# Gated attention: tiles' states side by side in four groups of the array's columns, logits with a block in each half of the columns

## The chip, the cores and the metric

The kernel runs on one core of one Trainium2 chip. The metric is the device time of one execution in microseconds (us); the median of several runs is compared. The core has TensorE (PE, with PEld for its weight loads), VectorE (DVE), ScalarE (ACT), GpSimd (POOL) and SyncE (SP), which issues most DMAs. A tile here is also 128 consecutive tokens; a block is 512 tokens, four tiles.

## The reference, cut to what matters

Two layers are computed, each an attention and a feed-forward part with residuals and layer norms. The change is in the second layer's attention, on 2 sequences of 1024 tokens with 512 channels, keys of 32 and values of 512:

```python
q = jax.nn.softmax(x @ Wq.T, axis=-1)            # [b, L, 32]
k = jax.nn.sigmoid(x @ Wk.T)
gf = jax.nn.log_sigmoid(-k)                       # log of the decay
# in chunks, with Bc the running sum of gf in the chunk:
A = tril(einsum('bid,bjd,bijd->bij', q, k, exp(Bi - Bj)))
o = A @ v + (q * exp(Bc)) @ S                     # v = x
S = S * exp(Blast)[..., None] + einsum('bjd,bjv->bdv', k * exp(Blast - Bc), v)
# then
go = o @ Wog.T + x @ Wig.T
x = layernorm(x + (rmsnorm(o) * go * sigmoid(go)) @ Wo.T)
```

All of it is in float32.

## The kernel before

One program of four stages. Stage 1 (to about 205 us) is the first layer's attention, stage 2 (to about 551 us) its feed-forward part with 4-bit weights, stage 3 (to about 757 us) the gated attention of the second layer, stage 4 its feed-forward part on the tokens that a router picks. The change touches the end of stage 2 and all of stage 3.

A framework turns the Python text into one queue of instructions for each engine: a scheduler orders them by priorities in program order and by its costs, `tc.issue_after(x)` asks that what follows be issued behind `x`, and every queue is then worked off in order, each instruction waiting on semaphores for what it needs. PSUM has eight banks of 128 x 512 floats, used in turn: `mm_bank` gives the next of four, `acc_bank` of the other four. `jk` is a pool with two buffers of 128 x 512 floats, given out in turn under the one tag `junk`; who takes a buffer waits until the readers of what it held are done.

The gated attention works in blocks 0 to 3 (`blk`), two for each sequence `b`:

- `turn(blk)` (L647) transposes the rows of a block on TensorE (`x2Tp`, one bank and one ACT copy a tile) to `xT[blk]`.
- `logits(b)` (L656) multiplies the transposed rows of a sequence's eight tiles with `wqk`, 64 columns (32 for q, 32 for k): eight tiles by four chunks of channels, 32 matmuls with 128 x 128 of `xT` stationary and 64 columns of `wqk` moving, into one bank `lp` (rows on partitions).
- `Gates` (L670) makes from `lp` the sigmoid `k`, the softmax `q`, `l` (negative log decay, by an exponential and a Ln, which need different ACT tables) and, with a matmul by the constant `suf` into `ep`, the decay to the end of a tile, `e`. `decayed` multiplies `e` and `k` to `kd`, written four times side by side (8 tiles x 4 x 32 columns).
- `front(blk)` (L1043) sums `l` along the tokens of four tiles at once by a matmul with `cm` into `cp`; the tiles' 32 key channels stand in the four quadrants of 32 partitions. ACT makes the exponentials `ex`. From the last column of `ex` DVE makes `last`, a matmul with `quads` spreads it over all quadrants (`dp`), and DVE copies the result to `decay`.
- `scores(blk)` (L1060) transposes `q` and `k` (`tp`), weights them on DVE (`km`, `kk`, `qm`, `qk`, `qi`), multiplies them (`sc`, 512 columns, and `sk`, whose stationary operand has 64 columns), masks the result to `A`, and makes the states: for each tile a matmul `up` of the 128 columns of `kd` (four copies of 32) with the tile's rows of `x`, 512 columns, and on DVE `S` = old `S` x `decay` + `up`, 128 x 512. So a tile's state stands in all four quadrants; `qi` of a tile is zero outside the tile's own quadrant.
- `attend(blk)` (L1113) makes the transposed output in four chunks of 128 channels, one bank `op` each: for each tile one matmul of `x` with `A` and one of the tile's `S` with `qi`, 128 columns each (the first tile of a sequence has no `S`). ACT copies each bank to `o` and squares it (`sq`, in a `jk` buffer); POOL adds the squares.
- `o_sum`, `other_sums`, `gate` (L1154) and `finish_by_seven` (L1237) make `go` and the final projection in the seven-product manner (products `go`, `grow`, `P`), `rms` the root mean square (`mp`), `scored_rows` the layer norm and the router's scores; `route` ranks them (`rp`, `cmp`).

The order of the parts is that of the loop at L1637 with `fillers` (L1622), and for the logits of sequence 0 that of the loop that ends stage 2 (`take(pieces, steps)`, the products `P` of the last block, with `turn(1)`, `logits(0)` and `decayed` between). Sequence 1's `turn(3)`, `logits(1)`, `Gates` and `decayed` stand together behind block 1's `rms`.

## Time and profile before

| | |
|---|---|
| median of 3 runs | 976.59 us (975.92 to 977.11) |
| the profiled execution | 977.26 us |
| its span, first to last instruction | 975.5 us |
| TensorE busy, share of the span | 961.5 us, 99% |
| TensorE weight loads | 776.4 us, 80% |
| DVE / ACT / POOL busy | 708.4 / 289.4 / 306.4 us |
| granted TensorE clock, mean | 0.998 |
| `op` matmuls, records: with A, with S | 128 and 112 |
| `lp`, `up`, `dp` matmuls, records | 128, 28, 8 |
| DVE updates of `S` in PSUM and SBUF | 12, median 0.746 us each |

The profile is of one execution, whose time is the span and 1.76 us around it. A matmul on 32-bit floats leaves two records on TensorE and two weight loads, a transposition one of each. The ends of matmuls are modelled and run into the next one, so that the distance from start to start, not the extent, is what a matmul takes of the queue.

### The profile page before, as it was taken

The page shows a single profiled execution, that of the slowest core. Times are in us where ns is not written, and L with a number is a line of the kernel's source. Part 1 is how long each engine was busy: PE and PEld are TensorE (multiplying, and loading weights), DVE is VectorE, ACT ScalarE, POOL GpSimd, SP SyncE. Part 2 cuts the span into 40 slices and gives each one's busy share as a digit, 9 for nine tenths or more (in the row PEclk, how much of TensorE's full clock was granted, in tenths as well). Part 3 has the DMA queues.
Part 4 walks back from the last instruction along what each step waited for, and adds up shares of the span by engine and source line. Part 5 has one row for each costly group of instructions (what it writes and reads, how often), then busy time and mean ns, then how long its engine had stood idle before and what let it go on. Part 6 is the DMA issues. An engine that isn't in the chain of part 4 may idle for free. (4 is left out here: it accounts for less than half of the span.)

```text
span 975.5 us, 11890 instructions
## 1 busy us (share of the span) xinstructions
PE 961.5 (99%) x4437; PEld 776.4 (80%) x4437; DVE 708.4 (73%) x1351; ACT 289.4 (30%) x496; POOL 306.4 (31%) x276
## 2 busy tenths in 40 slices
PE   8999999999999999999999999999999999999996
PEld 6668876775888888888889869969768688888886
DVE  2569986887985686676668386665897795898645
ACT  2244333342552263254242323233121133220000
POOL 1110183004887355575568012001033011000022
PEclk9999999999999999999999999999999999999999
DMA  9622212100000000000020320000004302140011
GB/s 323 209 75 88 88 56 75 53 1 0 2 1 1 1 1 1 1 1 0 1 75 13 136 102 1 2 0 1 1 32 142 130 13 75 44 173 0 1 44 44
DMA packets 25981, 48.88 MB, mean 50 GB/s; under 512 B 4684, under 2 KB 6732, under 8 KB 25411
## 3 DMA queue, kind: packets, MB, share of 16 engines
q1 hardware_dynamic: 23283, 42.98, 13.1%
q0 software_dynamic: 1920, 4.22, 1.1%
q10 hardware_dynamic: 720, 0.92, 0.4%
q8 instruction: 35, 0.57, 0.2%
q14 instruction: 23, 0.19, 0.1%
HBM read 39.70 MB, written 10.52 MB: 51 GB/s over the span
## 5 line engine op out<-in xcount | busy, mean ns | idle before, releaser
L181 POOL TENSOR_TENSOR rs<-rs,table 128x4 f32<-128x4 f32 (+1 forms) x21 | 19.7, 936 | 307.6 <-DVE rs L180 307.4
L741 DVE SCALAR_TENSOR_TENSOR gate<-gatep,scale,gate 128x512 f32<-128x512 f32 x123 | 91.3, 742 | 6.4 <-PE gatep L730 6.1
L741 DVE SCALAR_TENSOR_TENSOR up<-upp,scale,up 128x512 f32<-128x512 f32 x112 | 83.0, 741 | 0.1
L730 PE MATMUL gatep<-x1Th,wgu 128*128 128x512 f32 x176 | 72.5, 412 | 0.6 <-DVE x1Tl L212 0.6
L730 PE MATMUL upp<-x1Th,wgu 128*128 128x512 f32 x176 | 70.4, 400 | 0.1
L730 PE MATMUL upp<-x1Tl,wgu 128*128 128x512 f32 x176 | 68.9, 392 | 0.0
L730 PE MATMUL gatep<-x1Tl,wgu 128*128 128x512 f32 x176 | 68.9, 392 | 0.0
L735 ACT ACTIVATE gate<-gatep,scale 128x512 f32<-128x512 f32 x41 | 28.3, 691 | 110.4 <-PE gatep L730 104.0
L777 PE MATMUL P<-wdn,h 128*128 128x256 f32 x256 | 60.5, 379 | 0.0
L931 POOL TENSOR_TENSOR h<-up,gate 128x512 f32<-128x512 f32 x30 | 38.6, 1287 | 68.6 <-ACT gate L930 63.3
L777 PEld LDWEIGHTS P<-wdn,h 128*128 128x128 f32 x256 | 48.4, 190 | 6.7
L1133 POOL TENSOR_TENSOR sum<-sum,sq 128x512 f32<-128x512 f32 x12 | 17.3, 1442 | 90.7 <-issue 75.9
L1163 PE MATMUL go<-big 128*128 128x256 f32 x192 | 43.4, 380 | 0.0
L367 PE MATMUL xk<-pair,x 128*128 128x512 f32 x96 | 42.7, 592 | 0.0
L730 PEld LDWEIGHTS upp<-x1Th,wgu 128*128 128x128 f32 x176 | 33.0, 187 | 11.7 <-DVE up L741 3.4
L188 DVE BATCH_NORM_STATS2 st<-x 128x6 f32<-128x512 f32 x64 | 42.0, 674 | 0.4
L730 PEld LDWEIGHTS gatep<-x1Th,wgu 128*128 128x128 f32 x176 | 33.1, 188 | 9.2 <-DVE gate L741 1.8
L1163 PEld LDWEIGHTS go<-big 128*128 128x128 f32 x192 | 36.2, 190 | 4.8
L730 PEld LDWEIGHTS upp<-x1Tl,wgu 128*128 128x128 f32 x176 | 33.1, 188 | 6.4 <-issue 0.2
L730 PEld LDWEIGHTS gatep<-x1Tl,wgu 128*128 128x128 f32 x176 | 33.1, 188 | 6.0
L777 PE MATMUL P<-T,S 128*128 128x256 f32 x160 | 36.0, 379 | 0.0
L777 PEld LDWEIGHTS P<-T,S 128*128 128x128 f32 x160 | 30.3, 190 | 4.2
(486 smaller groups left out, 2327.3 us busy)
## 6 DMA issues: line engine op xcount, KB each, us to landing
pk<-in_gu SPq DMA_DIRECT2D x16, 352.0 KB, 3.7
x<-in_x SPq DMA_DIRECT2D x4, 1024.0 KB, 13.1
w<-in_w SPq DMA_DIRECT2D x1, 4096.0 KB, 14.5
xs<-picked SPq DMA_DIRECT2D x4, 1024.0 KB, 5.2
out<-x SPq DMA_DIRECT2D x4, 1024.0 KB, 4.3
w<-in_w SPq DMA_DIRECT2D x4, 1024.0 KB, 7.1
x0T<-in_xT SPq DMA_DIRECT2D x3, 1024.0 KB, 6.2
pk<-in_dn SPq DMA_DIRECT2D x11, 256.0 KB, 3.4
```

The source lines that it names most:

```text
L181: power = nc.gpsimd.tensor_tensor(rs[:, :n], rs[:, :n], const("mhalf")[:, :n], ALU.pow).ins
L188: nc.vector.bn_stats(st, x)
L367: ins = nc.tensor.matmul(acc_of[b][c], x_t[blk][:, i, c * P : (c + 1) * P], pairs_of["k", blk][i // 2][:, i % 2], start=blk % 2 == 0 and i ...
L730: ins = nc.tensor.matmul(ps, wgu[:, k, at * P : (at + 1) * P], x[:, k], start=x is parts[0], stop=x is parts[1]).ins
L735: nc.scalar.activation(acc, ps, AF.Copy, scale=s)
L741: last = nc.vector.scalar_tensor_tensor(acc, ps, s, acc, ALU.mult, ALU.add).ins
L777: last_p[0] = nc.tensor.matmul(cut, x(j)[:, r], w[:, j], start=j == 0, stop=j == NP - 1 and tail is None).ins
L931: hm = nc.gpsimd.tensor_mul(h.chunk(f), up, gate).ins
L1133: nc.gpsimd.tensor_add(sum2, sum2, sq)
L1163: ins = nc.tensor.matmul(ps[:, 256 * m : 256 * m + 256], w[:, k, m], b[:, k, 256 * half : 256 * half + 256], start=first and m == 0 and k ...
```

## The change

- The logits are made transposed: `wqk` (64 columns) is the stationary operand and 512 rows of a block move. The sequence's two blocks stand in the two halves of the array's columns and of one bank's partitions, `lT`, in turn chunk by chunk: 8 matmuls. ACT copies `lT` to SBUF, four transpositions bring it to `lp` (`turned_logits`), with the tiles of a bank in another order, which `Gates` reads by strides.
- `kd` is kept once (8 x 32 columns). A tile's `up` has 32 columns of `kd` stationary and goes to the quadrant of the next tile's number, so that the four (or three) tiles of a block share one bank `up` and stand in the array's four groups of 32 columns.
- A state is kept once, in the quadrant of its tile: `states[blk]` holds the four tiles' states side by side, so that DVE's update works on 32 partitions with the factor read from `ex` in place. `last`, `dp`, `decay` and the constant `quads` are gone. The state before a sequence's first tile is zero (a memset on POOL).
- `attend` multiplies all four tiles' states at once: one matmul of 512 columns for each chunk of channels, in place of four of 128.
- Order: the `ep` matmul moves from `Gates` to `decayed`. At the end of stage 2 the steps of `pieces` are split so that `logits(0)`, `turned_logits`, `Gates` and `decayed` stand further apart. For sequence 1, `turn(3)` moves into block 0's gating, `logits(1)` stands before block 1's `attend`, with `lT` in a `jk` buffer, `turned_logits` and `Gates` right behind it, and `decayed` between the first products of `finish_by_seven`, with `e` in a `jk` buffer. `fillers` is called once, before `sc`, with both halves.

TensorE's queue from the end of `attend`'s block 0 to the `up` of block 2, in words: `tp`, three matmuls `go`, three `up`, five `go`, `sc`, `sk`, 16 `go`, `mp`, 8 `go`, 16 transpositions `x2Tp`, 8 `go`, 8 `lT`, `op` of block 1, 4 `lp`, 4 `grow`, 4 `P`, 8 `go`, `ep`, 4 `grow`, 4 `P`, 8 `go`, 4 `grow`, 4 `P`, 4 `grow`, `mp`, `cp`, `tp`, 2 `go`, 4 `up`.

```diff
@@ -56,7 +56,6 @@
         "one": np.ones((P, 1)),
...
         "mhalf": np.full((P, 4), -0.5),
-        "quads": (tt % 32) == (ii % 32),
     }
...
     for name, a in parts.items():
@@ -653,51 +652,57 @@
             nc.scalar.copy(xT[blk][:, :, i * P : (i + 1) * P], pt.rearrange("p (k t) -> p k t", k=KC))
...
-    def logits(b):
+    def logits(b, room):
+        lT = mm_bank("lT")
+        for k in range(KC):
+            for g in range(2):
+                with tc.issue_after(last_turned[0]):
+                    last_turned[0] = nc.tensor.matmul(
+                        lT[64 * g : 64 * g + 64], wqk[:, k], xT[2 * b + g][:, k], start=k == 0, stop=k == KC - 1
+                    ).ins
+        nc.scalar.copy(room, lT)
+        return room
+    def turned_logits(lT):
         lp = mm_bank("lp")
-        for i in range(8):
-            for k in range(KC):
-                nc.tensor.matmul(
-                    lp[:, i * 64 : (i + 1) * 64],
-                    xT[2 * b + i // 4][:, k, (i % 4) * P : (i % 4 + 1) * P],
-                    wqk[:, k],
-                    start=k == 0,
-                    stop=k == KC - 1,
-                )
+        for i in range(4):
+            last_turned[0] = nc.tensor.transpose(lp[:, i * P : (i + 1) * P], lT[:, i * P : (i + 1) * P], ident).ins
         return lp
...
         def __init__(self, lp, rooms):
-            lg = lp.rearrange("p (i d) -> p i d", d=64)
-            self.q, self.k, self.l, self.e = q, k, l, e = rooms
-            nc.scalar.activation(k, lg[:, :, 32:], AF.Exp, scale=-1.0)
+            lg = lp.rearrange("p (i g d) -> p g i d", g=2, d=64)
+            self.q, self.k, self.l = q, k, l = rooms
+            q4, k4 = (x.rearrange("p (g i) d -> p g i d", g=2) for x in (q, k))
+            nc.scalar.activation(k4, lg[:, :, :, 32:], AF.Exp, scale=-1.0)
             nc.vector.tensor_scalar_add(k, k, 1.0)
...
             red = sp.tile([P, 8], F32, tag="red", name="red")
-            nc.vector.tensor_reduce(red, lg[:, :, :32], AX.X, ALU.max)
-            nc.vector.tensor_sub(q, lg[:, :, :32], red.unsqueeze(2).to_broadcast([P, 8, 32]))
+            red4 = red.rearrange("p (g i) -> p g i", g=2)
+            nc.vector.tensor_reduce(red4, lg[:, :, :, :32], AX.X, ALU.max)
+            nc.vector.tensor_sub(q4, lg[:, :, :, :32], red4.unsqueeze(3).to_broadcast([P, 2, 4, 32]))
             nc.scalar.activation(q, q, AF.Exp)
...
+        def decayed(self, kd, e):
             ep = mm_bank("ep")
-            nc.tensor.matmul(ep[:, :256], const("suf"), l.rearrange("p i d -> p (i d)"), start=True, stop=True)
+            ins = nc.tensor.matmul(
+                ep[:, :256], const("suf"), self.l.rearrange("p i d -> p (i d)"), start=True, stop=True
+            ).ins
             nc.scalar.activation(e.rearrange("p i d -> p (i d)"), ep[:, :256], AF.Exp)
-        def decayed(self, kd):
             self.kd = kd
-            nc.vector.tensor_mul(
-                kd, self.e.unsqueeze(2).to_broadcast([P, 8, 4, 32]), self.k.unsqueeze(2).to_broadcast([P, 8, 4, 32])
-            )
+            nc.vector.tensor_mul(kd, e, self.k)
+            return ins
...
         NP = (NI - 1) // 2
@@ -966,7 +971,7 @@
...
         W1oT = part(3, [4, 512])
-        kd_room, o_room = shaped(8192, [8, 4, 32]), shaped(9216, [KC, 512])
+        kd_room, o_room = shaped(8192, [8, 32]), shaped(9216, [KC, 512])
...
         gA11, gA12, gA21, gA22 = (
@@ -994,18 +999,26 @@
                 pass
...
             with tc.issue_after(mm), tc.issue_after(hm):
-                take(pieces, steps)
+                take(pieces, 3)
+            if n == 3:
+                with tc.issue_after(last_p[0]):
+                    lp = turned_logits(lT)
+                gate_rooms = [
+                    x[:, i * 256 : (i + 1) * 256].rearrange("p (i d) -> p i d", d=32) for x in (b2, rw) for i in range(2)
+                ]
+                gates = Gates(lp, gate_rooms[:3])
+            with tc.issue_after(mm), tc.issue_after(hm), tc.issue_after(last_turned[0]):
+                take(pieces, steps - 3)
             if n < 2:
...
             if n == 2:
-                gates = Gates(logits(0), [
-                    x[:, i * 256 : (i + 1) * 256].rearrange("p (i d) -> p i d", d=32) for x in (b2, rw) for i in range(2)
-                ])
+                lT = logits(0, rooms[1][0])
             if n == 3:
-                gates.decayed(kd_room)
                 sums_of_gate()
             if n == 4:
+                with tc.issue_after(last_p[0]):
+                    gates.decayed(kd_room, gate_rooms[3])
                 x_sum(0)
...
         W1o = place_w(1, "W1o")
@@ -1032,7 +1045,8 @@
     picked = [dram.tile([TOPK, ROW], F32, name=f"picked{b}") for b in range(B)]
...
     index = [cpool.tile([P, 8], I32, name=f"index{b}") for b in range(B)]
-    oT, uT, tri, state, inv = {}, {}, {}, {}, {}
+    oT, uT, tri, states, inv = {}, {}, {}, {}, {}
+    new_state = lambda: wk.tile([P, C], F32, tag="S", name="S", bufs=3)
...
     fronts = {}
@@ -1040,28 +1054,20 @@
     def of_tiles(x, blk):
...
-    def front(blk, gates, before=None):
+    def front(blk, gates):
...
         last_ex[0] = nc.scalar.activation(ex[:, 3], cp[:, :P], AF.Exp, scale=-1.0).ins
-        last = sp.tile([P, 4], F32, tag="own", name="last")
-        nc.vector.tensor_scalar_mul(last, const("heads")[:, P:], ex[:, 2, P - 1 :])
-        dp = mm_bank("dp")
-        with tc.issue_after(before()) if before else contextlib.nullcontext():
-            nc.tensor.matmul(dp[:, :4], const("quads"), last, start=True, stop=True)
-        decay = sp.tile([P, 4], F32, tag="decay", name="decay")
-        nc.vector.tensor_copy(decay, dp[:, :4])
-        fronts[blk] = ex, decay
+        fronts[blk] = ex
...
             front(blk, gates)
-        ex, decay = fronts[blk]
+        ex = fronts[blk]
...
         tp = mm_bank("tp")
@@ -1094,20 +1100,29 @@
         nc.vector.tensor_mul(A, sc.rearrange("p (i t) -> p i t", i=4), over(const("caus")))
...
         tri[blk] = A, qi
-        for i in range(4):
-            t = 4 * (blk % 2) + i
-            if t == 7:
-                continue
-            up = mm_bank("up3")
-            nc.tensor.matmul(up, gates.kd[:, t].rearrange("p r d -> p (r d)"), x_t[blk][:, i], start=True, stop=True)
-            S = wk.tile([P, C], F32, tag="S", name="S", bufs=4)
-            if t == 0:
-                ins = nc.vector.tensor_copy(S, up).ins
+        b, tiles = blk // 2, range(3 if blk % 2 else 4)
+        if blk % 2 == 0:
+            states[blk] = new_state()
+            nc.gpsimd.memset(states[blk][:32], 0.0)
+        up = mm_bank("up3")
+        quad = lambda x, i: x[32 * (i % 4) : 32 * (i % 4) + 32]
+        for i in tiles:
+            nc.tensor.matmul(
+                quad(up, i + 1), gates.kd[:, 4 * (blk % 2) + i], x_t[blk][:, i], start=True, stop=True
+            )
+        for i in tiles:
+            S = states[blk]
+            if i == 3:
+                S = states[blk + 1] = new_state()
+            new, old = quad(S, i + 1), quad(states[blk], i)
+            if blk % 2 == i == 0:
+                ins = nc.vector.tensor_copy(new, quad(up, i + 1)).ins
             else:
                 ins = nc.vector.scalar_tensor_tensor(
-                    S, state[blk // 2, t], decay[:, i : i + 1], up, ALU.mult, ALU.add
+                    new, old, quad(ex, i)[:, 2, P - 1 :], quad(up, i + 1), ALU.mult, ALU.add
                 ).ins
-            state[blk // 2, t + 1] = S
         return ins
...
     def attend(blk):
@@ -1119,11 +1134,13 @@
             op = mm_bank("op")
...
             for i in range(4):
-                S = state.get((blk // 2, 4 * (blk % 2) + i))
-                oi = op[:, i * P : (i + 1) * P]
-                nc.tensor.matmul(oi, x_t[blk][:, i, cut], A[:, i], start=True, stop=S is None)
-                if S is not None:
-                    nc.tensor.matmul(oi, S[:, cut], qi[:, i], start=False, stop=True)
+                nc.tensor.matmul(
+                    op[:, i * P : (i + 1) * P], x_t[blk][:, i, cut], A[:, i], start=i == 0, stop=False,
+                    skip_group_check=True,
+                )
+            last_op[0] = nc.tensor.matmul(
+                op, states[blk][:, cut], qi.rearrange("p i t -> p (i t)"), start=False, stop=True, skip_group_check=True
+            ).ins
             nc.scalar.copy(o[:, c], op)
...
                 nc.scalar.activation(sum2, op, AF.Square)
@@ -1149,7 +1166,7 @@
         nc.vector.tensor_sub(x[:, :, 256:], o[:, :, 256:], x[:, :, 256:])
...
-    last_3, last_ex = [None], [None]
+    last_3, last_ex, last_op = [None], [None], [None]
...
@@ -1619,14 +1636,15 @@
...
-    def fillers(h):
-        turn(2, (2 * h, 2 * h + 1))
-        next(gating)
+    def fillers():
+        for h in range(2):
+            turn(2, (2 * h, 2 * h + 1))
+            next(gating)
         return last_3[0]
-    front(0, gates, lambda: fillers(0))
-    scored = scores(0, gates, lambda: fillers(1))
+    front(0, gates)
+    scored = scores(0, gates, fillers)
     first_ex = last_ex[0]
...
     with tc.issue_after(first_ex):
@@ -1639,15 +1657,27 @@
             sums = sums_of_u()
...
             front(3, gates)
-        sum2 = attend(blk)
+        if blk == 1:
+            with tc.issue_after(last_3[0]):
+                lT = logits(1, jk.tile([P, 512], F32, tag="junk", name="lT"))
+        with tc.issue_after(last_turned[0]) if blk == 1 else contextlib.nullcontext():
+            sum2 = attend(blk)
+        if blk == 1:
+            with tc.issue_after(last_op[0]):
+                lp = turned_logits(lT)
+            last_3[0] = last_turned[0]
+            gates = Gates(lp, [wk.tile([P, 8, 32], F32, tag=n, name=n) for n in ("q3", "k3", "l3")])
         if blk:
...
                 finishing = finish_by_seven(blk - 1, sums, W1o_sums)
-                for _ in range(2):
+                for n in range(2):
                     next(finishing)
                     next(gating)
+                    if blk == 1 and n == 0:
+                        with tc.issue_after(last_3[0]):
+                            last_3[0] = gates.decayed(kd_room, jk.tile([P, 8, 32], F32, tag="junk", name="e3"))
                 next(finishing)
...
             else:
@@ -1659,13 +1689,6 @@
             ranking = route(0, xT_tile("row"))
...
             rms(blk, sum2)
-        if blk == 1:
-            turn(3)
-            gates = Gates(logits(1), [
-                *(wk.tile([P, 8, 32], F32, tag=n, name=n) for n in ("q3", "k3", "l3")),
-                jk.tile([P, 8, 32], F32, tag="junk", name="e3"),
-            ])
-            gates.decayed(kd_room)
         if blk < 3:
...
         if blk == 0:
@@ -1684,6 +1707,9 @@
         for n, done in enumerate(gating):
...
                 rms(0, sum2)
+            if n == 2 and blk == 0:
+                with tc.issue_after(last_3[0]):
+                    last_3[0] = turn(3)
             if n == 1 and blk < 3:
...
                     x_sum(blk + 1)
```

## Prediction

> **What bounds the kernel now.** I read the page first, then TensorE's timeline through the stretch that the change touches (520 to 720 us), then the same stretch on DVE, ACT and POOL.

> ```profile
> PE 961.5 (99%) x4437; PEld 776.4 (80%) x4437; DVE 708.4 (73%) x1351; ACT 289.4 (30%) x496; POOL 306.4 (31%) x276
> PEclk9999999999999999999999999999999999999999
> ```

> TensorE is busy for 99% of the span at full granted clock, so what the change adds to or takes from its queue moves the end one for one, unless another engine then ends last. The timeline gives the prices (start, extent, engine, line, operands, count of records, and in brackets an idle time and what ended it):

> ```profile
> 716.59 13.90 PE L1281 MATMUL ao<-W1o,uT 128*128 128x512 f32 x32
> 730.32 3.62 PE L1163 MATMUL go<-x2T,Wig 128*128 128x256 f32 x16
> 733.78 3.62 PE L1163 MATMUL go<-big 128*128 128x256 f32 x16
> ```

> A matmul leaves two records, a transposition one. The extents overlap, so I price by starts: 512 columns cost (730.32-716.59)/32 = 0.429 us a record, 256 columns (733.78-730.32)/16 = 0.216. In the same way 64 `op` records from 709.44 to 716.59 give 0.112 for 128 columns.

> ```profile
> 625.78 4.64 PE L661 MATMUL lp<-wqk,x2T 128*128 128x64 f32 x40
> 630.26 0.61 PE L197 MATMUL x2Tp<-table,x 128*128 128x128 f32 x4
> 630.70 2.79 PE L661 MATMUL lp<-wqk,x2T 128*128 128x64 f32 x24
> 633.33 3.67 PE L1163 MATMUL go<-big 128*128 128x256 f32 x16
> 636.84 2.75 PE L1163 MATMUL go<-big,Wog 128*128 128x256 f32 x12
> 640.11 0.70 PE L692 MATMUL ep<-l,table 128*128 128x256 f32 x2 [0.53 <-ACT l L681]
> ...
> 642.38 0.59 PE L1163 MATMUL go<-x2T,Wig 128*128 128x256 f32 x2
> 644.02 0.39 PE L1055 MATMUL dp<-last,table 128*128 128x4 f32 x2 [1.05 <-DVE last L1052]
> ```

> The logits' 64-column records take 0.112 each, as much as those of 128 columns: half the time goes to nothing but their weight loads. Behind them stand two of the waits that the change touches.

> **Part by part** (us on TensorE's queue, minus is a gain).

> Logits. Removed: 64 records twice, 523.76 to 530.85 (7.09) and 4.48+2.63 = 7.11, together 14.20. Added, twice: eight `lT` matmuls of 512 columns, alternating between the two halves of the columns, and four `lp` transpositions (4 x 0.11 = 0.44). What eight such matmuls cost is the open question. No row shows two matmuls in different columns at once. One end: none overlap, 16 records x 0.429 = 6.86. Other end: both records of one half run beside both of the other, 8 x 0.429 = 3.43. I take the case between. Records start in program order in every row, and a matmul's second record needs the columns of its first; but the second of one half and the first of the next hold different columns. So 16 records take 9 slots, 3.86. This is a judgement near the full end, since what spaces the shown rows is that they all share their columns.

> Each visit to narrower columns also costs, as `sk` (64 columns) shows:

> ```profile
> 561.43 1.02 PE L1090 MATMUL sc<-qm,km 128*128 128x512 f32 x2
> 562.38 0.65 PE L1092 MATMUL sk<-qk,kk 128*64 128x256 f32 x2
> 562.96 1.12 PE L1102 MATMUL up<-x,big 128*128 128x512 f32 x2
> ```

> `sc` to `sk` takes 0.95 and not 2 x 0.429 = 0.86; `sk` to `up` 0.58 and not 0.43; `up`'s first pair extends 1.12 where undisturbed pairs have 1.02. That is 0.34 per visit, say 0.35. [...] Logits: 2 x (3.86+0.35+0.44) = 9.30 against 14.20: **-4.90**.

> State products `up`. Removed: 562.96 to 566.50 (3.54), 1.75+0.86, 0.85+2.68 and 1.71+0.86, together 12.25. Added: 4, 3, 4 and 3 matmuls in different quarters. By the ends 8/6/8/6 slots (none overlap) or 2 each (all); by my rule 5+4+5+4 = 18 slots x 0.429 = 7.72, three visits at 0.35 and one at 0.12 that borders on `sk`: 8.89. **-3.36**. [...]

> Outputs `op`. Removed: 240 records x 0.112 = 26.8. Added: the 64 products with A unchanged (128 x 0.112 = 14.3), and 16 of S with 512 columns (32 x 0.429 = 13.7). The first tile of a sequence now multiplies a zero state. **+1.22**.

> `dp`, four times, with the disturbed record behind it: 0.14+0.22+0.25+0.32: **-0.93**.

> Waits that go, counted from where the records ahead would have ended by their spacing to the start of the late one: `dp` 642.38+0.43 to 644.02, 1.21; second `ep` 636.84+12 x 0.216 to 640.11, 0.68; likewise the first `ep` at 536.96, 0.44 (19 matmuls now lie between `lp` and `ep`, not 13), `sc` at 578.75, 0.69 and 0.11 for its exposed load (in front of `qm` DVE loses `last` and `decay`, 0.2, and by the new order 1.8 of a sum of `W1o` and statistics, which move behind), and `sc` at 696.47, 0.29+0.11 (six `go` matmuls stand ahead of it, not two: 1.7). **-3.53**. Late next at that last `sc` is still `qm`, 10.8 us after `mp` starts; TensorE now gets there after 0.81 (`mp`) + 0.25 (`tp`) + 22 `go` x 0.432 + 2.07 (`up`) = 12.6.

> The new wait is at the second `ep`. Its chain starts after `op` of block 1 and is covered by `lp` (0.44) and 32 records of `grow`, `P` and `go` (6.91): 7.35. The chain's prices:

> ```profile
> 607.17 2.28 DVE L1145 TENSOR_TENSOR big<-big 128x1024 f32<-128x1024 f32 x1
> 609.38 1.21 DVE L1149 TENSOR_TENSOR x2T<-big,x2T 128x1024 f32<-128x1024 f32 x1
> 634.49 1.74 DVE L679 RECIPROCAL k<-k 128x256 f32<-128x256 f32 x1
> ```

> ```profile
> 638.26 1.28 ACT L681 ACT_TABLE_LOAD   x1
> 639.55 0.51 ACT L681 ACTIVATE l<-l,table 128x256 f32<-128x256 f32 x1
> ```

> `lT` holds one of the two `jk` buffers until `lp` has read it, so ACT's square of the third `op` waits for that (0.44, and 0.2 from TensorE's last record to ACT). Then square 0.48, copy 0.48; DVE's `o_sum` and `other_sums`, ahead of the gates, follow the copy from 1.7 (2.21+1.14 by their starts): 5.1. The add, the maximum and the reciprocal (633.94 to 636.15) bring 7.3. Two exponentials 0.74, table load 1.28, Ln 0.51: 9.8, a wait of 2.5. Bounds: 0 (before, 6.8 from `lp` to `ep` including all this) and 5 (both sums slow, the load late). Queued behind it are `grow`, the sixteen `go` and the next `cp`; DVE and ACT wait with it. **+2.5**.

> At no cost: `turn(3)` moves ahead (16 records before and after); `kd` shrinks from 1024 to 256 elements and the S updates stay at 0.75 each, on DVE with slack beside TensorE; two copies of `lT` (0.59, `x2T`'s row) on ACT, covered by 1.3 us of `P` the first time and by `op` the second, and the full 0.6 each if that cover is gone; two small memsets on POOL ahead of `ms` and `sum`, which have us to spare. No DMA moves but a narrower table at the start.

> Sum: -4.90-3.36+1.22-0.93-3.53+2.5 = **-9.0**. The profiled execution took 977.26 (span 975.50, 1.76 around it), so 968.3; it was 0.67 above the median of the runs, 976.59, against which I forecast **967.6**. A difference under 0.2% (2.0 us) can't be told from no change here.

> **Rivals.**
> All columns run side by side: `up` needs 8 slots, `lT` 8 each, 10+2 slots or 5.1 us less: 962.5. Against it: program order of the records.
> No overlap: `lT` 14 slots more, `up` 10, so 24 x 0.429 = 10.3, and 977.9: no change that can be told. For it: not one pair of overlapping records in the trace.
> Slower: every column tile pays as `sk`'s entry does, 0.09 to drain and 0.03 to 0.05 of exposed load, 30 matmuls x 0.13 = 4, on top of no overlap: near 982. It decides for slower once overlap is absent and the price passes (978.5-977.9)/30 = 0.02 a matmul. For it: the entry's price in `sk`'s rows; against it: the load for `sk`'s second record runs beside its first (both loads fall within 0.19 us).

> **How the numbers follow.** Forecast 0.68 (965 to 970 by the new wait's bounds), side by side 0.08, no overlap 0.13, slower 0.11. The range 963.5 to 979.0 takes in the forecast's and no overlap's unknowns and leaves out about 0.19. Faster 0.76 (forecast, side by side); same 0.10 and slower 0.14, no overlap being split 0.10 to 0.03.

> **What would show it.** Starts of `lT` records 0.43 apart in pairs, 4.2 per group and not 7.2; `up` groups 2.1 and 1.7 and not 3.4 and 2.6; 32 records of `op<-qi,S` at 0.43; no `dp`; one wait of ACT `l` ahead of the second `ep`, 0 to 5. I am wrong if the groups show 16 and 8 slots, or if a wait of over 5 appears at `sc`, `op` or `ep`.

## The result, and the profile after

The changed kernel took **966.13 us**, median of five runs (965.79 to 967.52), beside 976.62 us of the kernel before on the same chip (975.92 to 977.11): a ratio of 0.9892, 95% interval 0.9881 to 0.9904. That is 10.5 us less, where the forecast said 967.6, 9.0 less. The profiled execution took 965.93 us, with a span of 963.8.

The profile's line for the engines, busy time, share and records, TensorE first:

```profile
PE 948.5 (98%) x4261; PEld 753.1 (78%) x4261; DVE 706.4 (73%) x1343; ACT 290.8 (30%) x498; POOL 310.5 (32%) x278
```

TensorE has 13.0 us less to do than before and still sets the end. Its timeline (start, extent, line, operands, records, idle time and what ended it) answers the question that the forecast left to a judgement, how matmuls in different columns share time:

```profile
523.03 3.65 PE L661 MATMUL lT<-x2T,wqk 128*64 128x512 f32 x16
526.61 1.56 PE L782 MATMUL P<-T,h 128*128 128x256 f32 x6
...
557.92 0.65 PE L1098 MATMUL sk<-qk,kk 128*64 128x256 f32 x2
558.49 1.07 PE L1112 MATMUL up<-x,big 128*32 128x512 f32 x8
559.49 0.91 PE L1060 MATMUL cp<-table,rw 128*128 128x384 f32 x2
```

From start to start `lT`'s eight matmuls take 3.58 us and `up`'s four take 1.00: little over eight and two slots of 0.429, where one after the other would be 16 and 8. The single records show how. The first records of the four `up` start within 20 ns of each other (558.493, .500, .507, .513), and the second records of all four start 0.454 us behind them, again within 20 ns. So the first record of the fourth matmul starts before the second record of the first one.

The price of the change is in the waits, which the timeline shows at two places:

```profile
585.57 1.95 PE L196 MATMUL x2Tp<-table,x 128*128 128x128 f32 x16
589.85 3.72 PE L1180 MATMUL go<-big,Wog 128*128 128x256 f32 x16 [2.34 <-DVE uT L1216]
...
608.09 3.62 PE L1180 MATMUL go<-x2T,Wig 128*128 128x256 f32 x16
613.53 0.70 PE L699 MATMUL ep<-l,table 128*128 128x256 f32 x2 [1.82 <-ACT l L685]
```

The second is the wait that I had forecast, at 2.5. The first I had not seen. A third, of 0.61, stands at 694.61, again for `uT` L1216. In TensorE's records from 515 us to the end of the group `ao` that starts at 704.50 (before: 716.59), the idle time rises from 2.54 us to 4.89.

### The profile page after: what moved, and what is told of

Same layout as the page of the kernel before. It is cut to its first block, busy times and chain, and to the rows that moved or that the text cites. A ratio compares the mean times of both kernels' runs of the same rounds, so it can differ in the third digit from the quotient of the medians.

```text
span 963.8 us, 11530 instructions
## 1 busy us (share of the span) xinstructions
PE 948.5 (98%) x4261; PEld 753.1 (78%) x4261; DVE 706.4 (73%) x1343; ACT 290.8 (30%) x498; POOL 310.5 (32%) x278
## 5 line engine op out<-in xcount | busy, mean ns | idle before, releaser
L1150 POOL TENSOR_TENSOR sum<-sum,sq 128x512 f32<-128x512 f32 x12 | 19.7, 1644 | 80.4 <-issue 66.3
```

Of the source, the lines that this page charges most:

```text
L1150: nc.gpsimd.tensor_add(sum2, sum2, sq)
```

## Experiments

Aligning TensorE's records of two profiles one by one gives the difference at each point. It also shows that the start varies: in the twelve profiles that follow, all with the narrower table, the matmuls just ahead of the change, at 510 us, lie between 0.15 us ahead of and 1.17 us behind those of the changed kernel's first profile (the kernel before: 0.84 behind). Differences "inside" leave that part out. By this measure the change is worth 11.25 us by 719 us and 10.8 at the end.

**The update over all columns.** Only the product is undone: four matmuls of 128 columns in four banks.

```diff
-        up = mm_bank("up3")
...
-            nc.tensor.matmul(
-                quad(up, i + 1), gates.kd[:, 4 * (blk % 2) + i], x_t[blk][:, i], start=True, stop=True
-            )
+            ups[i] = mm_bank("up3")
+            nc.tensor.matmul(ups[i], of_tiles(gates.kd, blk), x_t[blk][:, i], start=True, stop=True)
...
```

> Only the update's product is undone: each tile's update is again a matmul over all 128 columns of the array, into a bank of its own, with the four tiles' kd as its stationary side; the vector engine still takes only the tile's own quarter of it, and everything else is as in the changed kernel. Theory A (each group of columns runs as if it had a queue of its own, four tiles cost what one costs): a group of four goes from 1.00 us to 8 slots of 0.43 = 3.43 us, a group of three from 0.99 to 2.57, so 2 x 2.43 + 2 x 1.58 = 8.0 us more, about 974.2 us. Theory B, the forecast's rule (records start in program order, five and four slots a group): the changed kernel would have kept 2.15 and 1.72 us a group and this run would cost 4.3 us more. Theory C (the end is set elsewhere, TensorE's time here is covered): no change, 966.1 us.

Measured: 971.27 us (970.74 to 972.32), ratio to before 0.9942 [0.9926, 0.9959]; inside, 5.4 us more than the changed kernel. Theory A's price is there on TensorE's timeline, 3.54 us from start to start for four tiles that share nothing:

```profile
559.66 3.70 PE L1113 MATMUL up<-x,big 128*128 128x512 f32 x8
563.20 0.81 PE L1060 MATMUL cp<-table,rw 128*128 128x384 f32 x2
```

It does not all arrive: 8.0 us more matmul time, but with TensorE later the 2.34 us wait has gone, and so have two more of the same kind in later blocks, 0.61 and 0.42 (0.15 of it idle, the rest lateness by spacing), while `up` itself now waits 0.6 for VectorE. 8.0 - 2.3 - 0.6 - 0.4 + 0.6 = 5.3. Theories B and C are out.

**The update narrow, but in one quarter of the columns.**

```diff
...
-                quad(up, i + 1), gates.kd[:, 4 * (blk % 2) + i], x_t[blk][:, i], start=True, stop=True
+            nc.tensor.matmul(ups[i][:32], gates.kd[:, 4 * (blk % 2) + i], x_t[blk][:, i], start=True, stop=True)
...
```

> The update's matmuls stay 32 columns wide, but all of a group go to the same quarter of the columns (the first), each into a bank of its own; the vector engine reads them there. Theory A (time is shared only between different columns): they run one after the other, 8 and 6 slots of 0.43, 3.4 and 2.6 us a group, +8.0 us, about 974.2 us. Theory C (a narrow matmul is cheap by itself): 1.0 us a group as now, 966.1 us, and then the first quarter alone would have done it.

Measured: 972.71 us (972.70 to 973.10), 6.4 more inside. Four tiles take 3.55 us from start to start:

```profile
559.07 3.62 PE L1113 MATMUL up<-x,big 128*32 128x512 f32 x8
562.62 0.59 PE L1060 MATMUL cp<-table,rw 128*128 128x384 f32 x1
```

A narrow matmul alone was not cheaper, 3.55 us for four beside 3.54 at full width; the four took 1.00 where each lay in other columns than its neighbours. The run even costs about 1 us more than the full-width one: here as there the update's matmuls stand scattered among other products, so that the queue visits the narrow columns eight times and not four as in the changed kernel. A visit of one tile costs 0.09 in the matmul ahead (0.309 and not 0.216 to the next start), 0.12 in the group (0.98 for 0.86) and 0.10 in the matmul behind (0.320). That is about 0.3 for each of the seven visits that do not border on `sk`, some 2.2 in all; TensorE's idle time, 0.7 us shorter than in the full-width run, gives a part back, and the rest was not taken apart.

**Two quarters, in turn.**

```diff
...
-                quad(up, i + 1), gates.kd[:, 4 * (blk % 2) + i], x_t[blk][:, i], start=True, stop=True
+                quad(bank2, i % 2), gates.kd[:, 4 * (blk % 2) + i], x_t[blk][:, i], start=True, stop=True
...
```

> The update's matmuls take turns between two quarters of the columns, two banks a group. Theory A: two tiles side by side and two in turn, four slots of 0.43 plus 0.14 = 1.86 us for four tiles and the same for three, in place of 1.00 and 0.99: 4 x 0.87 = +3.5 us, about 969.6 us. Theory B (program order, a pair in three slots): six slots and five, 2.6 and 2.15 us, +5.5 us. Theory C: no change.

Measured: 967.70 us (967.37 to 967.93), 1.55 more inside. The first group takes 1.84 us from start to start, as theory A says (four slots of 0.429 and 0.12), and the shorter wait takes a part back here too: TensorE's waits for `uT` fall from 2.9 us in all to 0.9.

```profile
559.21 1.91 PE L1115 MATMUL up<-x,big 128*32 128x512 f32 x8
561.05 0.91 PE L1060 MATMUL cp<-table,rw 128*128 128x384 f32 x2
```

One, two and four quarters: 3.55, 1.84 and 1.00 us for the same four products.

**The halves of `lT` one after the other.** The order of the loops is turned round.

```diff
-        for k in range(KC):
-            for g in range(2):
+        for g in range(2):
+            for k in range(KC):
```

> Only the order of the eight matmuls of each lT changes: the four of the first half of the columns one after the other, then the four of the second half, in place of taking turns. Theory A with a deep queue for each group of columns: nothing changes, 3.6 us for each lT, 966.1 us. Theory A with a shallow queue (one or two matmuls ahead of the ones that run): the second half starts when the first one is in its last matmul or two, 14 to 15 slots of 0.43 = 6.0 to 6.4 us, twice +2.4 to +2.8, so 971 to 972 us. Theory B (records in program order, the first record of one half beside the second of the other): 15 slots, also about 972 us. Theory C (a matmul of 64 columns is cheap by itself, whichever columns it is in): 3.6 us, no change.

Measured: 972.01 us (970.19 to 972.03), 5.2 more inside, of which only 2 x 1.77 belong to `lT`:

```profile
523.87 5.42 PE L661 MATMUL lT<-x2T,wqk 128*64 128x512 f32 x16
529.22 1.13 PE L782 MATMUL P<-T,h 128*128 128x256 f32 x4
```

No theory had this size. 5.35 us is 12.5 slots, between 8 (theory A, deep queue) and 14 or 15 (shallow). The records tell why: the second half's first matmul, the fifth in the order, starts 6 ns behind the first half's third, and so ahead of the fourth. Its columns had been free for 1.77 us. It ran once three records ahead of it still waited (the third's second and both of the fourth), and not while four did; the second `lT` shows the same 1.77 us. So program order between columns does not hold (theory B is out), and yet the order matters: the changed kernel's turns are needed.

The other 1.7 us came from the clock. Behind the 2.34 us wait, this profile's windows (TensorE's busy time and records, then the other engines, then the granted clock) show:

```profile
590.00:592.00 2.00, 0.12 (x2) 0.00 (x0) 2.00 (x4) 0.86 (x2) 0.00 (x0) 1.00 0.00 0
592.00:594.00 2.00, 1.54 (x6) 1.35 (x7) 0.40 (x1) 0.63 (x1) 0.00 (x0) 0.87 0.00 0
594.00:596.00 2.00, 2.00 (x6) 1.53 (x6) 0.00 (x0) 0.00 (x0) 0.00 (x0) 0.50 0.00 0
596.00:598.00 2.00, 2.00 (x8) 1.41 (x7) 0.00 (x0) 0.10 (x1) 0.00 (x0) 0.78 0.00 0
598.00:600.00 2.00, 2.00 (x7) 0.61 (x7) 1.44 (x3) 0.50 (x1) 0.00 (x0) 1.00 0.00 0
```

TensorE stands from 590 to 592.5, restarts at full clock, and then has half of it for 3.4 us: products start 0.427 us apart, not 0.216.

**The changed kernel again.**

> The changed kernel as it is, beside the next three and a few runs of the kernel before, on the same chip. Expected: 966.1 us, some runs about 1.5 us above the others if the granted clock falls to half for some 3.4 us behind the 2.34 us wait, as the profile of the run with the halves apart shows; the first matmuls behind the loads 0.5 to 1.2 us later than in the first profile of this kernel, if the 0.84 us by which that profile was ahead there belonged to the run and not to the narrower table.

Measured: 967.16 us, median of four runs (965.43 to 967.78), ratio 0.9893 [0.9877, 0.9910]. The profiled run (967.78) starts 0.15 us later than the first profile, not 0.5 to 1.2. Inside, it is the first profile's up to the wait and 1.69 us later behind it, for the same reason:

```profile
588.00:590.00 2.00, 0.01 (x1) 0.01 (x1) 1.94 (x3) 0.42 (x2) 0.00 (x0) 0.99 0.00 0
590.00:591.00 1.00, 1.00 (x2) 0.83 (x3) 0.00 (x0) 0.60 (x1) 0.00 (x0) 0.50 0.00 0
591.00:592.00 1.00, 1.00 (x4) 0.81 (x3) 0.00 (x0) 0.00 (x0) 0.00 (x0) 0.50 0.00 0
592.00:593.00 1.00, 1.00 (x4) 0.82 (x3) 0.00 (x0) 0.00 (x0) 0.00 (x0) 0.50 0.00 0
593.00:594.00 1.00, 1.00 (x5) 0.83 (x5) 0.00 (x0) 0.00 (x0) 0.00 (x0) 0.81 0.00 0
594.00:595.00 1.00, 1.00 (x7) 0.86 (x5) 0.00 (x0) 0.00 (x0) 0.00 (x0) 1.00 0.00 0
```

So the wait costs its 2.34 us in each of these profiles and a further 1.7 in some. Of the five profiles that have this wait, three show the half clock behind it; of those without it, none shows any from 515 to 770 us.

The traces' records of the granted clock also tell these profiles apart. They lie on one grid of 3.413 us from the clock's first rise: in the profile of the kernel before it rises at 5.04 us and falls at 971.02, behind TensorE's last work, 283 such intervals later; in the changed kernel's first it rises at 5.71 and falls at 961.44, 280 later. In the changed kernel's second profile it rises at 6.29, falls at 589.97, 171 intervals later, and rises again one interval behind that. In this one the stand, 587.65 to 589.99, lies but for 0.02 us inside the interval just ahead of the fall, 586.56 to 589.97. The run with the halves apart agrees: TensorE stands from 590.12 to 592.46, and the clock has fallen at about 593.5, as the 0.87 from 592 to 594 says. In the first profile a boundary at 589.39 cuts the stand into 1.87 and 0.46 us, in the run with `ep` later, below, one at 589.37 into 1.18 and 1.16, and the clock stays full. So in these profiles an interval with 2.32 us of idle time was followed by half the clock, as were those with 2.90 and 3.41 at the ends of the kernel before and of the changed kernel's first profile; those with 1.87, 1.58 and 1.57 us in that first profile were followed by the full clock. The same wait of 2.34 us was caught in one profile of the changed kernel and missed in the other, by where it lay in this grid.

**The logits undone.** The old 32 matmuls a sequence, into `lp`, at `lT`'s place.

```diff
-        lT = mm_bank("lT")
+        lp = mm_bank("lp")
...
+                    last_turned[0] = nc.tensor.matmul(
+                        lp[:, at : at + 64],
+                        xT[2 * b + i // 4][:, k, (i % 4) * P : (i % 4 + 1) * P],
+                        wqk[:, k],
...
-        for i in range(4):
-            last_turned[0] = nc.tensor.transpose(lp[:, i * P : (i + 1) * P], lT[:, i * P : (i + 1) * P], ident).ins
...
```

> Only the logits are undone: 32 narrow matmuls of 64 moving columns a batch into lp, at the place where lT is now made, no turn back and no copy by ScalarE; the update, the output product and the order of the rest stay as in the changed kernel. In the kernel before the two groups took 14.20 us of TensorE's queue; in the changed one lT takes 2 x 3.59 us, lp 2 x 0.44 and the way into and out of the half width about 2 x 0.3, 8.7 us together. Theory A (this time is on the path): +5.5 us, 971.6 us. Theory B (without copy and turn the gates' chain starts earlier, which shortens the 1.82 us wait at ep): +3.7 to +5.5 us. Theory C (the logits are covered): no change.

Measured: 970.32 us (969.78 to 971.95), 4.2 above the first median of the changed kernel and 3.2 above the second. Its profile has the half clock too (0.79 between 592 and 600); the 1.7 us of that taken off, it is 5.9 behind the changed kernel where `op` and `lp` of block 1 are done and 3.8 from `ep` to the end. That is theory B: each group takes 7.09 us again where `lT` and `lp` take 4.02, but `ep` no longer waits, since the chain to `l` starts ahead of `op`'s 7 us and not behind them: on ScalarE, the `Ln` that makes `l` ends at 612.95, where `ep` starts at 619.64.

```profile
598.58 7.25 PE L662 MATMUL lp<-wqk,x2T 128*128 128x64 f32 x64
605.67 1.11 PE L1138 MATMUL op<-A,x 128*128 128x128 f32 x8
...
619.64 0.59 PE L700 MATMUL ep<-l,table 128*128 128x256 f32 x2
```

So the new logits save about 6 us of TensorE's queue and give 2 back at `ep`.

**The output product by tiles.**

```diff
...
-            last_op[0] = nc.tensor.matmul(
-                op, states[blk][:, cut], qi.rearrange("p i t -> p (i t)"), start=False, stop=True, skip_group_check=True
-            ).ins
+                last_op[0] = nc.tensor.matmul(
+                    op[:, i * P : (i + 1) * P], states[blk][:, cut], qi[:, i], start=False, stop=True
+                ).ins
```

> The output product takes the state tile by tile again, four matmuls of 128 columns for each of the four parts, with the whole of the state tile as their stationary side, in place of one of 512 columns. The moving columns are the same, 1024 a part. Forecast's rule (time goes by moving columns, the stationary side is loaded beside them): 7.2 us a block as now, no change, 966.1 us. Rival (three more loads of the same stationary side a part are seen): 48 loads of at most 0.11 us, up to +5 us.

Measured: 964.55 us (964.13 to 964.96), 1.4 *less* inside, which neither theory had. A block's `op` takes 0.14 us more (7.31 beside 7.17 in block 2); the forecast's rule holds nearly. In block 0 the first product with a state now stands earlier in the queue and waits for it:

```profile
562.67 0.46 PE L1140 MATMUL op<-qi,S 128*128 128x128 f32 x2 [1.18 <-DVE S L1123]
```

The scheduler's order of VectorE is also another one further on: the sum `uT` that TensorE waits for comes ahead of the scalings and of `x_sum`, and the 2.34 us wait is gone. The profit comes with this order, not with the product, and it points at the place to mend.

**A bank of its own behind the wait.**

```diff
-        nc.scalar.activation(c21, product(one, gA22, gT4, 0, False), AF.Silu)
+        six = acc_bank("go") if blk == 0 else one
+        nc.scalar.activation(c21, product(six, gA22, gT4, 0, blk == 0), AF.Silu)
```

> In block 0 alone the gate's product of gA22 and gT4 gets a bank of its own; in the changed kernel it takes over the bank of the product before it, and so TensorE stands for 2.34 us until VectorE has added that one to uT. Theory A (this wait is on the path and nothing else is late there): 2.3 us less at that place and at the end, 966.1 - 2.3 = 963.8 us, and the half clock that the run with the halves apart had just behind this wait can no longer come. Theory B (what follows waits for the same VectorE work anyway, so that the wait only moves to the next product): 966.1 us, with a wait of about 2 us a few matmuls later.

In this run and the next but one that product no longer adds to the sums which the old bank holds, so a quarter of the gate's values in block 0 lacks them; instructions and sizes are the same. Measured: 963.68 us (962.90 to 964.03), 2.6 less inside, 2.5 of it at this place (+0.53 ahead of it, -1.97 just behind it, -2.06 at the end). Theory A.

**`ep` one step later.**

```diff
-                    if blk == 1 and n == 0:
+                    if blk == 1 and n == 1:
```

> The second sum of the decays (ep) and what follows it are placed one step later in the order of block 1, behind the second pair of finishing and gate products. Theory A (TensorE stands 1.82 us for l and nothing else is late): 1.8 us less, 964.3 us. Theory B (the matmuls that now come earlier wait for ScalarE's and VectorE's sums instead, which were just in time): between 0 and 1 us less, 965.1 to 966.1 us, with a new wait at the products that fill ep's old place.

Measured: 966.41 us (965.04 to 966.84), no difference in the median. The profiled run, the 965.04, is 1.58 us shorter inside: the wait of 1.82 is gone and 0.25 came in its old place, for `x` L1272. Why the other runs are longer was not profiled; the half clock behind the wait that this kernel keeps, 1.7 us, would do it. Theory A holds for the profile, and the run with both mended, below, settles it.

**Both together**, the same two edits:

> The bank of its own and the later ep together. If the two waits are independent of each other (theory A of both): 966.1 - 2.3 - 1.8 = 962.0 us. If the time won at the first is lost at the second (ScalarE's chain to l starts from TensorE's products, so it should move with them): about 964 us.

Measured: 961.85 us (961.46 to 962.54), 4.2 less inside. The two waits add up.

**The sum put ahead on VectorE:**

```diff
             nc.vector.tensor_add(c12, c12, p3)
-            yield end(0)
-            yield p7()
+            yield (added := p7())
+            with tc.issue_after(added): ins = end(0)
+            yield ins
```

> Block 0's last steps are reordered on VectorE alone: the sum that TensorE waits for (uT L1216, behind the product with gS3) is put ahead of the two scalings of the first half of uT and of x_sum; TensorE's, ScalarE's and GpSimd's orders stay, and all is computed. Theory A (the wait of 2.34 us is one on VectorE's order): the sum starts at the end of the layernorm's four x, some 2.4 us earlier, the wait falls to about 0 to 0.3 us, the end comes 2.0 to 2.3 us earlier, about 963.9 us, and no run has the half clock. Theory B (the scalings that are now later are needed at once by what follows): the wait comes back at the products that read uT, 966 us.

Measured: 963.82 us (963.51 to 964.32), ratio 0.9864 [0.9848, 0.9880], 2.5 less inside. First VectorE's timeline of the changed kernel, then this run's, then TensorE's in this run:

```profile
584.83 1.91 DVE L182 TENSOR_SCALAR x<-x,mv,rs 128x512 f32<-128x512 f32 x4 [1.37 <-POOL rs L180]
586.66 1.41 DVE L1197 SCALAR_TENSOR_TENSOR uT<-big,gw,uT 128x512 f32<-128x512 f32 x2
587.99 1.22 DVE L993 TENSOR_TENSOR big<-x2T 128x1024 f32<-128x1024 f32 x1
589.12 0.68 DVE L1216 TENSOR_TENSOR uT<-uT,go 128x512 f32<-128x512 f32 x1
```

```profile
585.66 1.92 DVE L182 TENSOR_SCALAR x<-x,mv,rs 128x512 f32<-128x512 f32 x4 [1.37 <-POOL rs L180]
587.48 0.69 DVE L1216 TENSOR_TENSOR uT<-uT,go 128x512 f32<-128x512 f32 x1
588.08 1.23 DVE L993 TENSOR_TENSOR big<-x2T 128x1024 f32<-128x1024 f32 x1
589.21 1.42 DVE L1197 SCALAR_TENSOR_TENSOR uT<-big,gw,uT 128x512 f32<-128x512 f32 x2
```

```profile
586.39 1.95 PE L196 MATMUL x2Tp<-table,x 128*128 128x128 f32 x16
588.22 3.72 PE L1180 MATMUL go<-big,Wog 128*128 128x256 f32 x16
```

The sum came behind 1.41 + 1.22 us of work that TensorE did not wait for. Put ahead of it, it ends as the transpositions do, and TensorE goes on without an idle time in brackets. The half clock is not in its profile, and the runs lie within 0.8 us.

**Both mended**, the sum ahead and `ep` later:

> The reordered sum together with ep one step later. In the two earlier runs the later ep took 1.6 us off the profile. Theory A (the two waits add up): 966.1 - 2.2 - 1.6 = 962.3 us, the lowest of the kernels that compute all. Theory B (the gates' chain to l is late by as much as TensorE's products come earlier): 963.5 us.

Measured: **962.78 us** (962.73 to 962.93), ratio to before 0.9854 [0.9838, 0.9871], the fastest of those that keep these sums; 4.05 less inside than the changed kernel. Theory A: 2.47 and 1.58.

## Why the prediction was right, and where it was not

The sign and the mechanism in outline were right: matmuls in different columns overlap (four `up` in 1.00 us and not 3.54), TensorE's queue sets the end, and a wait opens at the second `ep` (1.82 us). The rule for how far they overlap was wrong, and one wait was not seen. The total is closer than its terms by luck: the two errors, about 6 us too little gain and 4 too little waiting, cancelled in great part. By TensorE's starts, inside:

| term | forecast | measured |
|---|---|---|
| logits | -4.90 | -6.15 |
| `up` | -3.36 | -8.29 |
| `op` | +1.22 | +1.16 |
| `dp` | -0.93 | -0.77 |
| waits, those gone and the new one | -1.03 | +2.8, as the rest of the sum (idle time +2.35; the rest was not taken apart, the visits to narrower columns are in it) |
| sum at 719 us | -9.0 | -11.25 |

- **The slots were mis-sized.** "Records start in program order" was the step that failed. It did not hold between columns: the fourth `up` starts 0.434 us before the first one's second record, and in the run with the halves apart the fifth `lT` before the fourth. Here a group takes the slots of its longest column, 2 and 8, and not 5, 4 and 9; the times named for it were 4.2 us at `lT` and 2.1 and 1.7 at `up`, and it takes 3.58, 1.00 and 0.99. That columns run side by side was the premise of the first rival, which had chance 0.08 and said 962.5. It failed in turn by leaving the waits as the forecast had them. The three tiles' 0.99 us stand in place of six slots, 2.57: a gain of 2.6.
- **The visits** cost what was said. At `lT` the last `go` ahead takes 0.309 us to the next start and not 0.216, the group 3.58 and not 8 x 0.429 = 3.43, and the first record behind the first group 0.320 and not 0.216: 0.35 together. At the third `up` the same three are 0.09, 0.14 and 0.10: 0.34. The slower rival's word for the 0.09 is draining; the rows show the distance, and not what TensorE does in it.
- **The wait at the second `ep`** was forecast at 2.5 with bounds 0 and 5, and is 1.82. Its chain is the forecast one but for the first link: the last copy of `op` did not stand behind a square that waits for `lp`, but ran at 604.40, so that VectorE began 0.8 us behind `op`'s end and not 1.7. Then come `o_sum` and `other_sums` on VectorE from 605.02 to 608.57, the reciprocal from 609.11, the exponential at 610.93, the table load and Ln to 613.5. The waits that were to go went, but for 0.23 us, and 0.10 of exposed load, at the `sc` of block 1 (its load starts 2 ns ahead of its first record, which takes 0.533 us to the next start and not 0.429).
- **"At no cost: `turn(3)` moves ahead" was wrong.** I counted its 16 records on TensorE's queue and not who then stands behind them. In the kernel before, matmuls of `op` stood among the last products of block 0's gate; now `op` is behind `lT`, the transpositions alone cover VectorE's sum, and TensorE comes earlier by what the update no longer takes. The rows of the kernel before, TensorE's and then the sum on VectorE:

```profile
591.11 3.62 PE L1163 MATMUL go<-x2T,Wig 128*128 128x256 f32 x16
594.56 0.38 PE L1126 MATMUL op<-qi,S 128*128 128x128 f32 x2
...
597.24 0.39 PE L1126 MATMUL op<-qi,S 128*128 128x128 f32 x2
597.46 3.62 PE L1163 MATMUL go<-big,Wog 128*128 128x256 f32 x16
```

```profile
595.20 0.68 DVE L1199 TENSOR_TENSOR uT<-uT,go 128x512 f32<-128x512 f32 x1
```

Counted from the start of the 16 `go` with `Wig`, the sum then ended at 4.8 us and TensorE wanted it at 6.35. In the changed kernel (from 582.01) it ends at 7.8, and TensorE is there at 5.5. So TensorE is there 0.85 us sooner, and the sum, behind the same two pieces of VectorE's work in both, ends 3.0 later. The covered wait came out at 2.34 us, with the half clock on top in some runs; the runs with the sum ahead and with a bank of its own show it worth 2.5 to 2.6. The same sum in the later blocks costs another 0.61 (at 694.61) and 0.42 (at 740.16).

- **The starts.** The first profile began its matmuls 0.84 us ahead of that of the kernel before. The profiles with the narrower table differ by 1.3 us among themselves, and no effect of the narrower table can be read from it.

Left open: what sets how far the array reaches past waiting matmuls, and what an interval with between 1.87 and 2.32 us of idle time does to the clock. The new order of the parts, the fewer calls of `fillers` and the lost `dp` were not undone by themselves; their shares are read from the timeline alone.

## What to carry to other kernels

Matmuls in different columns shared time here where they stood close in the queue: four in 1.00 us, where the same four in one quarter took 3.55. Price such a group by its longest column, as these runs measured it, but keep the columns in turn (`lT` took 3.58 us in turn, 5.35 with one half behind the other) and the group in one piece (each visit of a single tile cost about 0.3 us). When a change makes the bounding engine faster at one place, look at every wait that was covered there, by listing for each next product what its operand or bank waits for and what stands ahead of that on its own engine. Order alone can be worth a good part of a change: the sum's place on VectorE, busy for 73% of the span, and `ep`'s place on TensorE, edits that remove no work, are worth 4.05 us inside beside the change's 10.8, and brought 967.16 us down to 962.78 on the same chip, the half clock of some runs included.
